# Rearranging the last passes of a two-layer graph network: part of a normalisation moved ahead, two PSUM banks kept across stages, one product moved, one product undivided

## The chip, the cores and the metric

The kernel runs on one core of a Trainium2 chip. The metric is the device time of one execution in microseconds (us), lower is better; the time shown is the median of three runs. A profile is one execution recorded instruction by instruction. In it PE is TensorE's matmul, PEld its weight load, DVE VectorE, ACT ScalarE, POOL GpSimd and SP SyncE, which here only issues transfers.

## The reference

All data is fp32. The batch has 16 samples of 1024 nodes with 256 features.

```
# layer 0
h = maximum(layernorm(x), 0)
A = |  |sigmoid(mean_j - mean_i) - 0.5| - 0.5 | * 2        # mean over features of h
g = relu(h^T @ (adj * A) * para)                           # per sample, 1024 x 1024
k, v = split(h @ kv_w)
x = x + softmax(g^T k * scale) @ v                         # 4 heads of 64
# layer 1
h = maximum(layernorm(x), 0)
A_hat = (adj + I) * dinv[:, None] * dinv[None, :]
z1 = (A_hat @ h) @ W1.T + b1                               # 512 features
h2 = relu(batchnorm(z1))                                   # over all 16 x 1024 rows
z2 = h2 @ W2.T + b2                                        # 256 features
x = x + batchnorm(z2)                                      # over all rows again
```

The two batch normalisations are what stages the end of the kernel. Each needs sums over all 16 samples before its first value can be used.

## The kernel before, in words

The work is in two stages, each inside a block in which the program's own order is the order of every engine's queue (`tc.manual_schedule`). So each of TensorE, VectorE, ScalarE, GpSimd and SP does its instructions in the order in which the code names them, and an instruction that waits holds up everything behind it on its engine.

**Stage 1** (lines 171 to 1222) goes through the 16 samples. For each sample b it computes the graph product, attention (`attention`, L495), and then layer 1's first linear map for the sample before (`linear1_all`, L907: first `linear1`, L693, which multiplies with A_hat, then `linear1_seven`, L794, or for the very last sample `linear1_out`, L883). Both linear maps use a scheme of seven products of blocks for eight, so VectorE forms sums of blocks and ScalarE and VectorE combine the results. The products z1 go to memory in tiles of 512 nodes, `z1_d[t]` with t from 0 to 31, and their statistics for the batch normalisation to `st1`.

`linear1_all` takes hooks, functions that it calls between its products: `first` before the third, `second` after the fourth (`between[1]`, L753), `third` inside `linear1_seven` (`middle`, L861). In the last round (b = 15) these are the functions at L1180 to L1204. They put the layer normalisation of the last sample's x between the products of sample 14: statistics of row blocks 0 to 3 in `first`, of 4 to 7 in `third`, then `norm.invert` (a power on GpSimd for 1/sqrt, L257), a shift on VectorE (L263) and eight relus on ScalarE (L278). `left[3]` to `left[5]` are the last steps of attention. Behind them the products of sample 15 itself run.

[...]In stage 1 three pools hold them: `ps_s` (three buffers of two banks), `ps_o` and `ps_t` (one bank each), all opened at L172 to L174 and closed with the stage.

**Stage 2** (L1225 to L1579) makes z2 and the output. Its pools are opened over the banks that stage 1 left: `ps_x` with four banks and `ps_z` with four (L1246 to L1251). A tile in a bank of a closed pool waits for the last instruction that used the old pool there.

- Tiles t = 0 and 1 go through plain products (`begun`, `plain`, L1393 to L1408). The first half of their relus (`relu_on`, L149: the batch normalisation and the relu in one instruction) stands already in stage 1, between the evictions L900 of the last z1 tiles.
- Then 14 pairs of tiles (`SEVEN`, 1 to 14) go through class `Pair` (L1283), again seven products for eight. `m1`, `m6`, `m5` and `m3` add into one bank x in this order; after each, `keep` copies the sum to SBUF on ScalarE, and the next one waits for that copy. `m2`, `m7` and `m4` go to banks of `ps_z`; `add` and `out` add them on VectorE. While a pair is computed, ScalarE does the relus of the next one. In the last pair there is no next one, and ScalarE does the relus of the last two tiles, 30 and 31, instead (`relu_all`, L1429 and L1437).
- Tiles 30 and 31 then go through four plain products into banks of `ps_x` (L1476 to L1505), output half c = 0 first. Statistics come straight from PSUM. The very last product (tile 31, c = 1) is done in two halves of 256 columns, each with its own statistics; `triples` gathers them with the statistics of all other tiles.
- Meanwhile SP loads the samples' x1 again (`load_x1`, L1232), ten samples ahead in all, into tiles that the pairs have given back. When the second batch normalisation is known, ScalarE and VectorE scale z2, TensorE turns it (L1534), VectorE adds x1 (L1573), and ScalarE's queue stores the sample (L1574). Loads of samples 10 to 15 wait until stores give their tiles back.

Of the kernel before, what the change touches and what calls it, by code (L numbers as in the profile page):

```python
# [10 lines left out]
F32 = mybir.dt.float32  # L11
# [18 lines left out]
def fast_path(  # L30
# [135 lines left out]
    def relu(t, f2):  # L166
        zs[t, f2] = fetch(t, f2)
        relu_on(zs[t, f2], f2)


    with ExitStack() as stage:
        ps_s = stage.enter_context(tc.tile_pool(name="fps_s", bufs=3, space=PSUM))  # L172
        ps_o = stage.enter_context(tc.tile_pool(name="fps_o", bufs=1, space=PSUM))
        ps_t = stage.enter_context(tc.tile_pool(name="fps_t", bufs=1, space=PSUM))  # L174
        big = stage.enter_context(tc.tile_pool(name="fbig", bufs=1))
        two = stage.enter_context(tc.tile_pool(name="ftwo", bufs=2))
        w4 = stage.enter_context(tc.tile_pool(name="fw4", bufs=5))
# [868 lines left out]
        with tc.manual_schedule(engines={ENG.PE, ENG.Activation, ENG.DVE, ENG.Pool, ENG.SP}):  # L1046
# [73 lines left out]
            for b in range(B):  # L1120

                hooks = {}
                if b + 1 < B:
                    for c in range(2):
                        hooks.setdefault(c, []).append(lambda c=c: weights(b + 1, c))
                    if b == 0:
                        for m in range(NC):
                            hooks.setdefault(m // 2, []).append(lambda m=m: column_sums(m))
                        hooks[3].append(roots)
                else:  # L1130
                    w2n = lasting.tile([P, CC, F1], F32, tag="w2n", name="f_w2n")
                    nc.sync.dma_start(w2n, W2.rearrange("(c p) f -> p c f", p=P))
                left = attention(b, *qkv, hooks)

                def more(c):
                    return lambda: weights(b + 1, c)

                norm = Norm(xr[b], f"b{b}")
                between = {
                    0: [  # L1140
                        lambda: turn_h(b + 1), more(2), left[0], left[1], left[2], more(3),
                        left[3], left[4], more(4),
                    ],
                    1: [more(5)],
                    2: [more(6), lambda: norm.stats(0, 4)],
                    3: [more(7)],
                    4: [left[5], lambda: norm.stats(4, NC), norm.invert],
                    6: [lambda: norm.relu(0, 4)],
                    "late": [lambda: norm.relu(4, 6), lambda: norm.relu(6, NC)],
                    8: [lambda: leave(b), lambda: arrive(b + 2)],  # L1150
                }
                if b == 0:
                    scale = [lambda m=m: scale_adj(m) for m in range(NC)]
                    between[3].insert(0, roots_row)
                    between[4] = scale[:3] + between[4] + [scale[3]]
                if b + 1 < B:
                    if 0 < b < B - 2:
                        thirds = load_thirds(b)
                    qkv = graph(b + 1, between)
                    if b == 0:  # L1160
                        for step in scale[4:]:
                            step()
                        thirds = make_thirds(b)
                if b + 2 < B:
                    linear1_all(
                        b,
                        norm.h,
                        thirds,
                        lambda: prepare_start(b + 2),
                        lambda: prepare_end(b + 2),  # L1170
                        lambda: (prepare_row(b + 2), again(b + 1)),
                    )
                elif b + 1 < B:
                    kept_h = norm.h
                    again(b + 1)
                else:

                    w2T = lasting.tile([P, FC, C], F32, tag="w2T", name="f_w2T")

                    def first():  # L1180
                        norm.stats(0, 4)
                        left[3]()
                        left[4]()

                    def second():
                        pass

                    def third():
                        left[5]()
                        norm.stats(4, NC)  # L1190
                        norm.invert()
                        for n, (pool, tag) in enumerate(((ps_o, "o"), (ps_t, "t"))):
                            ps = pool.tile([P, 2, CC, P], F32, tag=tag, name=f"f_w2ps_{n}")
                            for d in range(2):
                                for f in range(CC):
                                    nc.tensor.transpose(
                                        ps[:, d, f, :], w2n[:, f, ts(2 * n + d, P)], ident
                                    )
                            nc.scalar.copy(
                                w2T[:, 2 * n : 2 * n + 2, :].rearrange("p d c -> p (d c)"),  # L1200
                                ps.rearrange("p d f q -> p (d f q)"),
                            )
                        norm.relu(0, NC)
                        leave(b)  # L1204

                    for step in left[:3]:
                        step()
                    thirds = load_thirds(b)
                    def nothing():
                        pass  # L1210

                    made = []
                    linear1_all(
                        b - 1,
                        kept_h,
                        thirds,
                        first,
                        second,
                        third,
                        lambda: made.extend(sums_of_h(b, norm.h)),  # L1220
                    )
                    linear1_all(b, norm.h, thirds, nothing, nothing, nothing, made=made)


    with ExitStack() as stage:  # L1225
# [16 lines left out]
        with tc.manual_schedule(engines={ENG.PE, ENG.Activation, ENG.DVE, ENG.Pool, ENG.SP}):  # L1242
            bn1.affine(FC - 2, FC)

            z2 = big.tile([P, CC, B - 1, N], F32, tag="z2", name="f_z2")
            ps_x = stage.enter_context(tc.tile_pool(name="fps_x", bufs=4, space=PSUM))  # L1246
            zps = ExitStack()
            ps_z = zps.enter_context(tc.tile_pool(name="fps_z", bufs=4, space=PSUM))

            def bank(name, pool=None):  # L1250
                return (pool or ps_z).tile([P, 512], F32, tag="z", name=name)  # L1251
# [138 lines left out]
                    relu_on(zs[t, f2], f2)  # L1390

            pairs = {p: Pair(p) for p in SEVEN}
            begun = {t: [bank(f"f_z2ps_{t}_{c}") for c in range(CC)] for t in (1, 0)}  # L1393
            first = pairs[SEVEN[0]]
            first.load()
            for t in range(2):
# [11 lines left out]
                plain_out(t, begun[t])  # L1408
            first.m1()
            first.keep(0, 0)  # L1410
            for p in SEVEN:
                now, soon = pairs[p], pairs.get(p + 1)
                if p + 2 in pairs:
# [19 lines left out]
                if soon:  # L1433
                    soon.relu(1, 1)
                    soon.relu(1, 0)
                else:
                    relu_all(TT - 1)  # L1437
                now.m5()
                now.keep(1, 1)
                if soon:  # L1440
                    soon.sums13()
                    soon.m1()
                    soon.keep(0, 0)
                now.out(1)
                now.m3()
                now.keep(1, 0)
# [10 lines left out]
            load_x1(AHEAD - 1, [(lasting, "w2n", 1), (io, "x1", None)])  # L1457
            zps.close()
            ps_out = stage.enter_context(tc.tile_pool(name="fps_out", bufs=2, space=PSUM))
            last = {}  # L1460

            triples = big.tile([P, 6, 3], F32, tag="triples", name="f_triples")
            SPLIT = TT // 2
            for k, n in enumerate((SPLIT, TT - 1 - SPLIT)):
                nc.vector.memset(triples[:, k, 0:1], float(n * 512))
# [9 lines left out]
            gather(0, 0, SPLIT)  # L1475
            for c in range(CC):  # L1476
                for t in range(TT - 2, TT):
                    ps = bank(f"f_z2ps_{t}_{c}", ps_x)
                    last[t % 2, c] = ps
                    if c + 1 < CC or t + 1 < TT:  # L1480
                        product(ps, t, c, 0)
                        product(ps, t, c, 2)
                        nc.vector.bn_stats(st2[:, c, t, :], ps)
                        continue
                    gather(1, SPLIT, TT - 1)
                    for k in range(2):
                        at = slice(256 * k, 256 * (k + 1))
                        for f in range(FC):
                            nc.tensor.matmul(
                                ps[:, at],  # L1490
                                w2T[:, f, ts(c, P)],
                                zs[t, f - f % 2][:, f % 2, at],
                                start=(f == 0),
                                stop=(f == FC - 1),
                            )
                        nc.vector.bn_stats(
                            triples[:, 2 + 2 * k : 4 + 2 * k, :].rearrange("p k s -> p (k s)"),
                            ps[:, at],
                        )
                bn2.invert(  # L1500
                    c,
                    c + 1,
# [591 lines left out]
```

## Time and profile before

| | |
|---|---|
| median of 3 runs | 2431.84 us (2431.0 to 2432.97) |
| the profiled execution | 2431.68 us, of which the span is 2429.8 us |
| PE busy | 2387.0 us, 98% of the span |
| DVE, ACT, POOL busy | 1781.9, 1325.6, 308.2 us |
| granted TensorE clock, mean | 0.995 |
| moved by DMA | 275.77 MB, 113 GB/s over the span |
| last products of stage 1 begin | 2124.49 us |
| first product of stage 2 begins | 2163.90 us |
| last product ends; first store is issued | about 2363; 2367.66 us |

Times of instructions are counted from the start of the span. One matmul of the code is two rows in the trace, so a product of 128 x 512 with four matmuls is eight rows. In a row of the timeline, the number in brackets is how long the engine was idle before it, and behind the arrow stands what released it. An "xN" merges N instructions that follow each other.

### The profile page before, as it was taken

The numbers are of one execution on the slowest core, as the hardware profiler recorded it, in microseconds if no ns is written. First come the engines' busy times: TensorE is split into PE (matmuls) and PEld (weight loads), VectorE is DVE, ScalarE is ACT, GpSimd is POOL, SyncE is SP. The second block draws the span as 40 slices with busy tenths as digits, with TensorE's granted clock in tenths as the row PEclk, the third lists the DMA queues.
The fourth block names the chain that finished last, engine by engine and source line by source line (L and its number), as shares of the span: only waits on it lengthen the run. The fifth ranks groups of instructions, "written<-read, shape, count | busy, mean of one in ns | idle before, by whom it ended". The sixth has DMA issues, their size and how long they took to land.

```text
span 2429.8 us, 24669 instructions
## 1 busy us (share of the span) xinstructions
PE 2387.0 (98%) x8042; PEld 1053.3 (43%) x8042; DVE 1781.9 (73%) x2441; ACT 1325.6 (55%) x1932; POOL 308.2 (13%) x546
## 2 busy tenths in 40 slices
PE   8999999999999999999999999999999999999995
PEld 4453444434343434444343434344443434444444
DVE  6878677685949586776859595867768596757766
ACT  6845555464636455554546364545545465346653
POOL 2030202020020302020201103020202010000000
PEclk9999999999999999999999999999999999999997
DMA  5041414232331415142323224141423212355569
GB/s 186 9 140 61 152 61 126 87 91 73 116 94 60 144 61 152 61 126 87 102 67 114 91 63 142 61 151 61 126 87 110 67 61 76 110 209 178 174 225 379
DMA packets 176634, 275.77 MB, mean 113 GB/s; under 512 B 37872, under 2 KB 121328, under 8 KB 176496
## 3 DMA queue, kind: packets, MB, share of 16 engines
q1 hardware_dynamic: 156336, 241.55, 30.6%
q0 software_dynamic: 15552, 15.77, 2.5%
q10 hardware_dynamic: 4608, 16.78, 1.7%
q8 instruction: 66, 1.08, 0.2%
q14 instruction: 72, 0.59, 0.1%
HBM read 169.35 MB, written 71.10 MB: 99 GB/s over the span
## 4 chain that ended last, share of the span: by engine, by line
PE 96%; DMA 2%; DVE 1%; ACT 0%; issue 0%; SPq 0%; POOL 0%; DVEq 0%; ACTq 0%; POOLq 0%
PE f_s L506 19%; PE f_o L547 18%; PE f_gps L398 18%; PE f_aps L703 16%; PE f_zps L809 6%; PE f_vps L423 5%; PE f_zx L1317 4%; PE f_zm L1317 3%; PE f_kpsx L467 2%; PE f_kps L467 1%; DMA out_dram<-f_x1t 1%; PE f_z2ps L1255 1%; PE f_zps L891 1%; PE f_kps L440 1%; PE f_zps3a L809 0%; PE f_zps3b L809 0%
## 5 line engine op out<-in xcount | busy, mean ns | idle before, releaser
L514 ACT ACTIVATE f_p<-f_s 128x1024 f32<-128x1024 f32 x512 | 477.3, 1048 | 150.2 <-PE f_s L506 150.1
L523 DVE TENSOR_TENSOR f_acc<-f_acc,f_p 128x1024 f32<-128x1024 f32 x384 | 470.5, 1225 | 41.1 <-ACT f_w L345 0.5
L506 PE MATMUL f_s<-f_qT,f_kT 64*128 64x512 f32 x2048 | 456.8, 596 | 0.0
L547 PE MATMUL f_o<-f_p,f_v 128*64 128x512 f32 x2048 | 453.6, 595 | 0.0
L398 PE MATMUL f_gps<-f_w,f_h_a 128*128 128x512 f32 x1024 | 444.7, 594 | 0.3 <-DVE f_w L336 0.3
L368 POOL DMA_DIRECT2D f_hT<-f_hQ x480 | 235.8, 499 | 1220.0 <-PE f_gps L398 1170.8
L506 PEld LDWEIGHTS f_s<-f_qT,f_kT 64*128 64x128 f32 x2048 | 190.8, 186 | 263.5 <-ACT f_p L514 117.0
L398 PEld LDWEIGHTS f_gps<-f_w,f_h_a 128*128 128x128 f32 x1024 | 192.8, 190 | 247.0 <-issue 230.7
L547 PEld LDWEIGHTS f_o<-f_p,f_v 128*64 128x64 f32 x2048 | 141.4, 137 | 304.3 <-issue 254.4
L349 DVE SCALAR_TENSOR_TENSOR f_w<-f_w,f_adj 128x1024 f32<-128x1024 f32 x127 | 153.9, 1212 | 38.8 <-ACT f_w L348 38.8
L345 ACT ACTIVATE f_w<-f_row,f_col 128x1024 f32<-128x1024 f32 x127 | 147.0, 1158 | 31.2 <-DMA f_row<-frow 30.2
L278 ACT ACTIVATE f_h_b<-f_x,f_shift_b,f_rstd_b 128x256 f32<-128x256 f32 x128 | 67.8, 594 | 160.9 <-DVE f_shift_b L263 160.9
L348 ACT ACTIVATE f_w<-f_w 128x1024 f32<-128x1024 f32 x127 | 134.3, 1058 | 4.0
L703 PE MATMUL f_aps<-f_ahatT,f_hs 128*128 128x512 f32 x256 | 115.1, 592 | 0.0
L703 PE MATMUL f_aps<-f_ahatT,f_h_b 128*128 128x512 f32 x256 | 112.7, 593 | 0.8 <-DVE f_z L865 0.8
L423 PE MATMUL f_vps<-f_kvw,f_hT 128*128 128x256 f32 x512 | 113.4, 379 | 0.0
L703 PE MATMUL f_aps<-f_t,f_hs 128*128 128x512 f32 x256 | 112.5, 592 | 0.0
L278 ACT ACTIVATE f_h_a<-f_x,f_shift_a,f_rstd_a 128x256 f32<-128x256 f32 x126 | 73.8, 587 | 63.5 <-DVE f_shift_a L263 63.4
L423 PEld LDWEIGHTS f_vps<-f_kvw,f_hT 128*128 128x128 f32 x512 | 97.2, 190 | 20.3 <-issue 7.4
L520 DVE TENSOR_TENSOR f_acc<-f_p,f_p 128x1024 f32<-128x1024 f32 x64 | 76.3, 1192 | 15.3 <-ACT f_p L514 15.3
L589 ACT COPY f_recs<-f_rec 32x32 f32<-32x32 f32 x128 | 31.5, 246 | 98.7 <-DVE f_rec L581 97.5
L574 ACT COPY f_parts<-f_red 32x64 f32<-32x64 f32 x128 | 39.1, 306 | 78.5 <-DVE f_red L539 77.4
(227 smaller groups left out, 2709.7 us busy)
## 6 DMA issues: line engine op xcount, KB each, us to landing
f_t<-ft SPq DMA_DIRECT2D x84, 512.0 KB, 6.9
fz<-f_z SPq DMA_DIRECT2D x64, 512.0 KB, 9.6
f_x<-in_x_dram SPq DMA_DIRECT2D x31, 1024.0 KB, 8.1
f_zb<-fz SPq DMA_DIRECT2D x42, 512.0 KB, 4.3
f_para<-in_L_gnn_para_dram SPq DMA_DIRECT2D x32, 512.0 KB, 4.5
f_att<-f_oT SPq DMA_DIRECT2D x512, 32.0 KB, 1.9
fx<-f_x SPq DMA_DIRECT2D x16, 1024.0 KB, 6.3
f_x1t<-fx SPq DMA_DIRECT2D x32, 512.0 KB, 7.3
```

What stands on the lines that cost most here:

```text
L345: nc.scalar.activation(w, rows[b], AF.Abs, bias=cols[b][:, c : c + 1], scale=0.5 / C)
L349: nc.vector.scalar_tensor_tensor(w, w, 1.0, adj_t[c], ALU.subtract, ALU.mult)
L368: queue.dma_start(to[ts(k, 32), ts(a, 32 * NC)], t[ts(a, 32), k].rearrange("i c r -> i (c r)"),)
L398: nc.tensor.matmul(gps[d][:, ts(g, 512)], hs[b][:, c, ts(d, P)], w[:, ts(g, 512)], start=(c == 0), stop=(c == NC - 1),)
L423: nc.tensor.matmul(ps[:, i, :], hT[e][:, ts(c4 + i, P)], kvw_t[:, e, C : 2 * C], start=(e == 0), stop=(e == CC - 1),)
L506: nc.tensor.matmul(ps[:, e, :], kT[rows_e, pair, ts(m, P)], qT[rows_e, pair, ts(g, 512)], start=True, stop=True,)
L514: nc.scalar.activation(p, ps, AF.Exp)
L523: nc.vector.tensor_add(acc_of[s], acc_of[s], p)
L547: nc.tensor.matmul(o_of[s][e * HD : (e + 1) * HD, :], v[:, m, ts(2 * pair + e, HD)], p[:, e, :], start=(m == 0), stop=(m == NC - 1),)
L703: nc.tensor.matmul(ps, left[:, m, :], right(m), start=not more and m == 0, stop=(m == KH - 1), skip_group_check=more,)
L809: nc.tensor.matmul(ps[i], left[:, ts(i, P)], right, start=not more, stop=True, skip_group_check=more,)
L1317: nc.tensor.matmul(ps, left[:, m, :], right[:, m, :], start=start and m == 0, stop=(m == 1), skip_group_check=not start,)
```

## The change

Four edits, all between the last sample's layer normalisation and the last batch normalisation.

1. The inversion of row blocks 0 to 3 moves from `third` to `first`, and their shift and their four relus to `second`. `third` keeps the other four row blocks.
2. `ps_o` and `ps_t` are opened outside stage 1 and stay open in stage 2; `ps_x` has two banks in place of four. Tile 0's two plain products go to `ps_o` and `ps_t` (`aside`), tile 1's to `ps_z`.
3. In the last pair, tile 31's relus move from ahead of `m5` to behind `keep(1, 1)`, and the first of the four last products (tile 30, c = 0) moves from behind the pair to between `m5` and `m3`. It goes to `ps_o`, the one of tile 31, c = 0 to `ps_t`, the other two to `ps_x`.
4. The last product is done in one piece, with one instruction for its statistics, and `triples` has four entries in place of six.

On SP the order of the instructions is the same as before. TensorE has two product instructions and VectorE one statistics instruction less for edit 4; VectorE and GpSimd have an addition, a shift and a power more for edit 1.

```diff
+    ps_o = ctx.enter_context(tc.tile_pool(name="fps_o", bufs=1, space=PSUM))
+    ps_t = ctx.enter_context(tc.tile_pool(name="fps_t", bufs=1, space=PSUM))
     with ExitStack() as stage:
         ps_s = stage.enter_context(tc.tile_pool(name="fps_s", bufs=3, space=PSUM))
-        ps_o = stage.enter_context(tc.tile_pool(name="fps_o", bufs=1, space=PSUM))
-        ps_t = stage.enter_context(tc.tile_pool(name="fps_t", bufs=1, space=PSUM))
...
                     def first():
                         norm.stats(0, 4)
+                        norm.invert(0, 4)
                         left[3]()
                         left[4]()
                     def second():
-                        pass
+                        norm.shifts(0, 4)
+                        norm.relu(0, 4, False)
                     def third():
                         left[5]()
                         norm.stats(4, NC)
-                        norm.invert()
+                        norm.invert(4, NC)
...
-                        norm.relu(0, NC)
+                        norm.shifts(4, NC)
+                        norm.relu(4, NC, False)
                         leave(b)
...
-            ps_x = stage.enter_context(tc.tile_pool(name="fps_x", bufs=4, space=PSUM))
+            ps_x = stage.enter_context(tc.tile_pool(name="fps_x", bufs=2, space=PSUM))
...
-            begun = {t: [bank(f"f_z2ps_{t}_{c}") for c in range(CC)] for t in (1, 0)}
+            def aside(name):
+                return [
+                    ps_o.tile([P, 512], F32, tag="o", name=f"{name}_0"),
+                    ps_t.tile([P, 512], F32, tag="t", name=f"{name}_1"),
+                ]
+            begun = {0: aside("f_z2ps_0"), 1: [bank(f"f_z2ps_1_{c}") for c in range(CC)]}
...
+            last = {}
+            def last_product(t, c, ps):
+                last[t % 2, c] = ps
+                for f2 in range(0, FC, 2):
+                    product(ps, t, c, f2)
...
                     soon.relu(1, 0)
-                else:
-                    relu_all(TT - 1)
                 now.m5()
                 now.keep(1, 1)
                 if soon:
                     soon.sums13()
                     soon.m1()
                     soon.keep(0, 0)
+                else:
+                    relu_all(TT - 1)
+                    ends = aside("f_z2ps_end")
+                    last_product(TT - 2, 0, ends[0])
                 now.out(1)
                 now.m3()
                 now.keep(1, 0)
...
-            triples = big.tile([P, 6, 3], F32, tag="triples", name="f_triples")
+            triples = big.tile([P, 4, 3], F32, tag="triples", name="f_triples")
...
                 for t in range(TT - 2, TT):
-                    ps = bank(f"f_z2ps_{t}_{c}", ps_x)
-                    last[t % 2, c] = ps
+                    if (t % 2, c) not in last:
+                        last_product(t, c, ends[1] if c == 0 else bank(f"f_z2ps_{t}_1", ps_x))
                     if c + 1 < CC or t + 1 < TT:
-                        product(ps, t, c, 0)
-                        product(ps, t, c, 2)
-                        nc.vector.bn_stats(st2[:, c, t, :], ps)
+                        nc.vector.bn_stats(st2[:, c, t, :], last[t % 2, c])
                         continue
                     gather(1, SPLIT, TT - 1)
-                    for k in range(2):
-                        at = slice(256 * k, 256 * (k + 1))
-                        for f in range(FC):
-                            nc.tensor.matmul(
-                                ps[:, at],
-                                w2T[:, f, ts(c, P)],
-                                zs[t, f - f % 2][:, f % 2, at],
-                                start=(f == 0),
-                                stop=(f == FC - 1),
-                            )
-                        nc.vector.bn_stats(
-                            triples[:, 2 + 2 * k : 4 + 2 * k, :].rearrange("p k s -> p (k s)"),
-                            ps[:, at],
-                        )
+                    nc.vector.bn_stats(
+                        triples[:, 2:4, :].rearrange("p k s -> p (k s)"), last[t % 2, c]
+                    )
```

More of the change, by code (lines that the diff above doesn't have):

```diff
@@ L1459, in fast_path @@
             ps_out = stage.enter_context(tc.tile_pool(name="fps_out", bufs=2, space=PSUM))
-            last = {}
-            triples = big.tile([P, 6, 3], F32, tag="triples", name="f_triples")
+            triples = big.tile([P, 4, 3], F32, tag="triples", name="f_triples")
             SPLIT = TT // 2
```

## The prediction, made before the changed kernel was run

> **What bounds the kernel now.** I read the chain of waits first, because it says which engine carries the end.
>
> ```profile
> PE 96%; DMA 2%; DVE 1%; ACT 0%; issue 0%; SPq 0%; POOL 0%; DVEq 0%; ACTq 0%; POOLq 0%
> ```
>
> 96% of the span is TensorE working or being waited for by itself, so only two things can move the time here: a hole in TensorE's row, or the transfers after it. I then read TensorE alone in order of time from 2080 us on, where the edits lie, and looked for holes.
>
> ```profile
> 2124.49 7.11 PE L703 MATMUL f_aps<-f_ahatT,f_h_b 128*128 128x512 f32 x16 [0.83 <-DVE f_z L865]
> ...
> 2148.60 13.90 PE L891 MATMUL f_zps<-f_aggT,f_w1T 128*128 128x512 f32 x32
> 2163.90 14.00 PE L1255 MATMUL f_z2ps<-f_z,f_w2T 128*128 128x512 f32 x32 [1.40 <-ACT f_z L900]
> ...
> 2341.17 1.88 PE L1317 MATMUL f_zx<-f_zb,f_w2s 128*128 128x512 f32 x4
> 2344.82 1.99 PE L1317 MATMUL f_zx<-f_zb,f_w2s 128*128 128x512 f32 x4 [1.77 <-ACT f_z L1328]
> 2346.64 1.88 PE L1317 MATMUL f_zm<-f_zt,f_w2T 128*128 128x512 f32 x4
> 2348.35 10.46 PE L1255 MATMUL f_z2ps<-f_z,f_w2T 128*128 128x512 f32 x24
> 2358.65 1.89 PE L1489 MATMUL f_z2ps<-f_z,f_w2T 128*128 128x256 f32 x8
> 2361.07 1.99 PE L1489 MATMUL f_z2ps<-f_z,f_w2T 128*128 128x256 f32 x8 [0.52 <-DVE f_triples L1496]
> ```
>
> Columns: start, busy us, engine, line, operation, then in brackets the idle time and its releaser. There are exactly four holes before the output stage: 0.83, 1.40, 1.77 and 0.52 us. One matmul of the code is two rows here; 24 rows take 2358.65 - 2348.35 = 10.30 us, so a row is 0.429 us and one 128x512 product (four matmuls) 3.43 us. A modelled end runs on past the next start, so I count holes by rows: 2148.60 + 32 x 0.429 = 2162.33, and the second hole is really 1.57 us; in the same way the third is 2344.82 - (2341.17 + 1.72) = 1.93 us.
>
> The first hole hangs on VectorE, which sits behind GpSimd's power:
>
> ```profile
> 2119.73 0.17 DVE L256 TENSOR_SCALAR f_var_b<-f_mv_b 128x8 f32<-128x8 f32 x1
> 2121.72 0.17 DVE L263 SCALAR_TENSOR_TENSOR f_shift_b<-f_mv_b,f_rstd_b 128x8 f32<-128x8 f32 x1 [1.81 <-POOL f_rstd_b L257]
> 2121.80 1.22 DVE L864 TENSOR_TENSOR f_z<-f_z,f_zps 128x1024 f32<-128x1024 f32 x1
> 2123.13 1.22 DVE L865 TENSOR_TENSOR f_z<-f_z,f_zps 128x1024 f32<-128x1024 f32 x1
> ```
>
> L864 and L865 need nothing from the shift; they only stand behind it. The third hole is on ScalarE:
>
> ```profile
> 2339.65 0.58 ACT L1328 COPY f_z<-f_zx 128x512 f32<-128x512 f32 x1 [1.74 <-PE f_zx L1317]
> 2340.13 1.52 ACT L152 ACTIVATE f_z<-f_z,f_bn_t,f_bn_s 128x512 f32<-128x512 f32 x2
> 2342.78 1.52 ACT L152 ACTIVATE f_z<-f_z,f_bn_t,f_bn_s 128x512 f32<-128x512 f32 x2 [1.13 <-DMA f_z<-fz]
> 2344.20 0.56 ACT L1328 COPY f_z<-f_zx 128x512 f32<-128x512 f32 x1
> ```
>
> The copy at 2344.20 is keep(1, 1), which TensorE's m3 waits for; it stands behind the relus of the last tile, whose data landed at 2342.78. After the products, transfers decide, as windows of 5 us show (last two columns: busy share of the DMA engines, GB/s):
>
> ```profile
> 2355.00:2360.00 5.00, 5.00 (x16) 2.71 (x15) 3.61 (x9) 1.52 (x2) 0.55 (x1) 1.00 1.04 413
> 2360.00:2365.00 5.00, 3.41 (x19) 2.52 (x17) 2.11 (x10) 3.11 (x3) 0.55 (x1) 1.00 0.85 315
> 2365.00:2370.00 5.00, 3.28 (x24) 2.57 (x24) 4.16 (x6) 2.77 (x3) 0.00 (x0) 1.00 0.63 235
> ...
> 2375.00:2380.00 5.00, 4.09 (x32) 3.42 (x32) 4.88 (x6) 3.01 (x3) 0.00 (x0) 1.00 1.02 397
> ```
>
> Loads of x1 fill the engines until about 2361; a dip follows until the first stores (2367.66); from 2375 to 2425 every window is at 397 to 420 GB/s. So the end is the start of the stores plus a fixed amount of traffic.
>
> [...]both halves of the last product are in one bank, and the trace shows the second half waiting 0.52 us for the first half's statistics. [...]0.52 granted from 2390 to 2405 among holes of 1.8 to 3.3 us, while the holes above left it at 1.00.
>
> **The change, part by part.**
>
> *A. Half of the relus ahead.* Statistics of the first four row blocks exist at 2096. The change inverts them there and runs four relus (8 took 4.04, so 2.0 us) on ScalarE after the shift. The shift stands on VectorE behind L752 (2100.51 + 0.69); its power was done near 2097, so VectorE doesn't stall on it; the relus run from about 2101.4 to 2103.5, in ScalarE's idle 5.25 us before L755 at 2103.94. Cover gone, L755 would be late, but its reader on TensorE comes 3.43 us later: nothing. In the late part GpSimd's power is 4 wide instead of 8: the two 4-wide ones at the start of this trace took 1.05 us, the 8-wide here 1.64. Shift, L864 and L865 move up by 0.58, L865 ends at 2123.77, TensorE starts at 2123.91. The last old row ends at 2122.64 + 2 x 0.429 = 2123.50, so 0.4 of the hole stays. The copy L868 behind the relus comes 2.5 us earlier, so it isn't late. Gain 0.58; bounds 0.3 and 0.99.
>
> *B. Two banks kept.* Before, the first z2 matmul takes over banks of pools that have just closed, and waits for the last eviction L900 (2162.59 + 1.26). With ps_o and ps_t alive its tile waits for its own relu alone: ScalarE's two relus from 2161.08 end by 2162.60, the first half near 2161.85, before TensorE is free at 2162.33; the second half is needed 0.86 later. Hole gone: 1.57. What is late next, in the times of before with the hole closed (A moves all of it alike): tile 1's matmuls begin two products' halves later, at 2165.76, and its relus and its banks, which still wait for L900, are ready at 2165.25; tile 0's second half is wanted at 2169.19 and 2170.05, its relus end near 2168.7 and at 2169.45; m1 begins at 2176.06 and m2 at 2177.78, and pair 1's relus end at 2176.55. ScalarE's four copies then end at 2178.52 and keep(0, 0) at 2179.1, where m6 wants it at 2179.5. All fit, the narrowest by 0.4 us. Pair 1's loads wait on VectorE's aggregate (SP issues them at 2166.54), not on TensorE, and land just ahead of ScalarE, as before. ps_x with two buffers for four costs nothing: a pair's bank is free one whole pair (12 us) before it is taken again. Gain 1.57; bounds 0.6 (the first pair gives a microsecond back) and 1.57.
>
> *C. Product between copy and relus.* keep(1, 1) now follows m5 directly, and TensorE has 3.43 us of product (tile 30's relus ended at 2337.9) while ScalarE copies (0.58) and does tile 31's relus (3.0). Both are over before m3 and the second product need them; tile 31's data has landed by then. The product is only moved, so its time is saved nowhere else. The hole of 1.93 goes, and 0.10 of restart (m3's four rows took 1.82 for 1.72). Gain 2.03; bounds 1.5 and 2.03. Its bank in ps_o was last read by tile 0's copies, 160 us before.
>
> *D. Last product in one piece.* Before: from the end of the third product, 2358.65, to the final aggregate at 2363.57 is 4.92 us (two halves, 0.52 of hole, two restarts, statistics 0.43). After: 3.43 + 0.21 until VectorE starts (as at 2351.99) + 0.74 until the next (as 2355.42 to 2356.16) = 4.38. Gain 0.54; bounds 0.3 and 0.7. The wider statistics instruction costs 0.27 and is in this sum. VectorE is free: tile 30's second statistics and gather end 1.6 us before.
>
> Sum of the stores' start: 0.58 + 1.57 + 2.03 + 0.54 = 4.72 us. SP's queue keeps its order. Its loads of x1 follow the last z load, which waits for m2 of the last pair (2337.97), so they start only A + B = 2.15 earlier; the four that reuse the last z tiles come 3 to 5 earlier, as their products do. The 2.57 between loads and stores is taken from the dip: missing rate in 2360 to 2370 is (100 + 180) x 5 / 415 = 3.4 us. It holds. Some 0.5 us of loads may still run when stores begin, and can cost up to that.
>
> Profiled execution: 2431.68 (span 2429.8), less 4.72, is 2426.96; the median of the runs is 0.16 higher, so 2427.1.
>
> **The rivals.**
> 1. *First pair gives B back.* ScalarE's row is solid from 2167.99 to 2178.52 and its loads land just ahead; then TensorE stalls at m2 or m6 for what B saved. For it: margins of 0.4. Against: ScalarE idled 1.13 us before keep(0, 0). 2427.1 + 1.57 = 2428.7.
> 2. *Transfers decide.* If stores gain nothing on the loads, the end moves by 2.15: 2429.7. For it: DMA at 1.03 in the tail. Against: the dip of 3.4 us.
> 3. *More than the sum*: A's hole closes wholly (0.4 more) and C and D save more of the restarts (0.3): 2426.4. Against it: L865's end at 2123.77, by rows that the trace shows.
> 4. *Slower.* [...]the trace holds 17 us at half clock in the tail. If such a stretch fell into the products instead, it would cost 8.5 us: 2427.1 + 8.5 = 2435.6. [...]the change only removes holes there, and holes up to 1.93 left the clock at 1.00. Unlikely.
> That an edit does nothing is open only for B; in the built program its wait is on the relu and no longer on L900.
>
> **How the numbers follow.** Forecast 0.66, rivals in order 0.12, 0.08, 0.09, 0.05. Time 2427.1. The range 2426.0 to 2429.8 holds all but rival 4 and tails. 0.2%, about what a measurement of this kernel can tell, is 4.86 us, a line at 2426.98: the forecast straddles it, so I give it 0.32 faster and 0.34 same. Faster: 0.32 + 0.09 = 0.41. Same: 0.34 + 0.12 + 0.08 + 0.01 = 0.55. Slower: 0.04, most of rival 4.
>
> **What would show it.** A: power 1.05 us, next hole about 0.4. B: first f_z2ps row with no idle time before it. C: m3 directly after a product. D: one row group of 512 columns. Then first stores near 2363, and the dip about 1 us. It is wrong if f_zm or f_zx rows of the first pairs show idle time over 0.5 us, or the stores start earlier and the end doesn't.

## The result, and the profile after

| | before | after |
|---|---|---|
| median of 22 runs each | 2432.19 us (2430.5 to 2434.8) | 2427.43 us (2425.95 to 2429.78) |
| profiled execution (span) | 2431.68 (2429.8) us | 2427.43 (2425.5) us |
| first products of the last linear map begin | 2124.49 us | 2122.78 us |
| stage 2's first product begins | 2163.90 us | 2160.65 us |
| loads of x1, from sample 1 on, begin | 2338.33 us | 2334.98 us |
| TensorE's row that starts with the first store | 2367.68 us | 2361.72 us |

The ratio is 0.998, 95% interval 0.9974 to 0.9986: 4.76 us less, with 3.4 to 6.3 in the interval. In the profile of after, the chain of waits still ends in TensorE:

```profile
PE 96%; DMA 2%; DVE 0%; issue 0%; SPq 0%; ACT 0%; ACTq 0%; DVEq 0%; POOLq 0%; POOL 0%
```

TensorE in order of time, with the places of the four old holes:

```profile
2122.78 7.13 PE L704 MATMUL f_aps<-f_ahatT,f_h_b 128*128 128x512 f32 x16
...
2146.92 13.90 PE L892 MATMUL f_zps<-f_aggT,f_w1T 128*128 128x512 f32 x32
2160.65 13.90 PE L1259 MATMUL f_z2ps<-f_z,f_w2T 128*128 128x512 f32 x32
...
2339.53 3.60 PE L1259 MATMUL f_z2ps_end<-f_z,f_w2T 128*128 128x512 f32 x8
2342.97 1.88 PE L1321 MATMUL f_zx<-f_zb,f_w2s 128*128 128x512 f32 x4
2344.68 1.88 PE L1321 MATMUL f_zm<-f_zt,f_w2T 128*128 128x512 f32 x4
2346.40 3.60 PE L1259 MATMUL f_z2ps_end<-f_z,f_w2T 128*128 128x512 f32 x8
2349.83 7.03 PE L1259 MATMUL f_z2ps<-f_z,f_w2T 128*128 128x512 f32 x16
2356.70 1.04 PE L1541 MATMUL f_outps<-f_ident,f_z 128*128 128x128 f32 x8
2359.75 1.09 PE L1541 MATMUL f_outps<-f_ident,f_z 128*128 128x128 f32 x8 [2.02 <-DVE f_z L1523]
2361.72 4.38 PE L1541 MATMUL f_outps<-f_ident,f_z 128*128 128x128 f32 x24 [0.88 <-DVE f_x1t L1580]
```

None of the rows from 2122.78 to 2349.83 has a bracket: the holes of 0.83, 1.40, 1.77 and 0.52 us are gone. 2160.65 - 2146.92 = 13.73 us is exactly 32 rows of 0.429, so even the half hidden part of the second hole went. What stands out is the last row: 24 transposes take 4.38 us there, where a row of 16 took 2.22 in before:

```profile
2367.68 2.22 PE L1534 MATMUL f_outps<-f_ident,f_z 128*128 128x128 f32 x16 [0.88 <-DVE f_x1t L1573]
```

This row starts with the first store: both wait for VectorE's first addition of x1 (the store is issued at 2367.66 before and 2361.70 after).

Not all of the 5.96 us between these two rows is the change's. A row of 16 matmuls in `linear1` for sample 14 (f_t, f_hs, at 2093.44 before and 2092.52 after) stands ahead of every edited instruction and is already 0.92 us earlier; over the profiles of this study it lies between 2092.30 and 2093.66. So below I count from that row, the *mark*. From the mark, the first store's row came 5.04 us earlier (269.20 for 274.24), and the start of the loads 2.43.

The transfers, in the windows of before (the last three columns: granted clock, busy share of the DMA engines, GB/s):

```profile
2355.00:2360.00 5.00, 2.98 (x15) 1.74 (x14) 2.23 (x8) 3.82 (x5) 0.55 (x1) 1.00 1.02 408
2360.00:2365.00 5.00, 4.12 (x24) 3.79 (x22) 3.58 (x3) 2.88 (x3) 0.00 (x0) 0.66 0.90 358
2365.00:2370.00 5.00, 4.38 (x34) 3.43 (x32) 4.77 (x5) 2.61 (x3) 0.00 (x0) 1.00 0.83 247
2370.00:2375.00 5.00, 3.87 (x30) 3.27 (x31) 4.88 (x6) 1.87 (x3) 0.00 (x0) 1.00 1.03 349
2375.00:2380.00 5.00, 2.63 (x21) 1.97 (x20) 4.88 (x5) 2.36 (x3) 0.00 (x0) 1.00 1.02 412
```

The dip is still there. Counted from 2360 to 2380 as rate missing to 415 GB/s (both profiles hold 410 to 420 in every window from 2380 to 2415) it is (57 + 168 + 66 + 3) x 5 / 415 = 3.5 us, against (100 + 180 + 77 + 18) x 5 / 415 = 4.5 in the same windows of before. And the clock is at 0.66 in the window in which the stores begin, where before had 1.00.

### The profile page after: what moved, and what is told of

It reads as the page before. It is cut to its first block, busy times and chain, and to the rows that moved or that the text cites. A ratio compares the mean times of both kernels' runs of the same rounds, so it can differ in the third digit from the quotient of the medians.

```text
span 2425.5 us, 24656 instructions
## 1 busy us (share of the span) xinstructions
PE 2385.3 (98%) x8034; PEld 1052.4 (43%) x8034; DVE 1781.4 (73%) x2442; ACT 1325.2 (55%) x1932; POOL 308.5 (13%) x547
## 4 chain that ended last, share of the span: by engine, by line
PE 96%; DMA 2%; DVE 0%; issue 0%; SPq 0%; ACT 0%; ACTq 0%; DVEq 0%; POOLq 0%; POOL 0%
PE f_s L507 19%; PE f_o L548 19%; PE f_gps L399 18%; PE f_aps L704 16%; PE f_zps L810 6%; PE f_vps L424 5%; PE f_zx L1321 4%; PE f_zm L1321 3%; PE f_kpsx L468 2%; PE f_kps L468 1%; DMA out_dram<-f_x1t 1%; PE f_z2ps L1259 1%; PE f_zps L892 1%; PE f_kps L441 1%; PE f_zps3b L810 1%; PE f_zps3a L810 1%
```

## The experiments

My theory was that of the prediction: the end follows the stores' start one for one, and the four gains add up. The rival: transfers decide, so only what starts the loads of x1 earlier (A and B) counts. Each kernel but the last (e12) is the changed one with one edit; e8 has none and e10 two. Medians scatter by about 1.5 us in an interval, as much as an edit is worth, so I read single edits from TensorE's rows as well. "Second transposes" is the row of 8 that VectorE's last scaling releases, at 272.27 us from the mark before and 267.23 after.

### Undoing one part

**e1, without A.**
```diff
-                        norm.invert(0, 4)
...
-                        norm.shifts(0, 4)
-                        norm.relu(0, 4, False)
+                        pass
...
-                        norm.invert(4, NC)
+                        norm.invert()
...
-                        norm.shifts(4, NC)
-                        norm.relu(4, NC, False)
+                        norm.relu(0, NC)
```


> The changed kernel with edit 1 undone (all eight relus late). Two theories of the end stand against each other in these four runs. Stores: the end moves one for one with the start of the stores, so each undone edit costs its own hole. Traffic: the end moves with the start of the x1 loads, and the dip between loads and stores takes up whatever comes after that. Here both say: the hole of about 0.8 us behind VectorE's L866 is back before the last products of stage 1 and everything after it is 0.8 later than in the changed kernel; time about 0.8 above it, some 4.0 below the kernel before (ratio 0.9984). The hole before the first f_z2ps row stays away.

Measured 2428.87 us, ratio 0.9986 (0.9979 to 0.9992). The old hole is back, 0.83 us behind VectorE's L866, and the second transposes come 0.75 us later than in after.

**e2, without B.**
```diff
-    ps_o = ctx.enter_context(tc.tile_pool(name="fps_o", bufs=1, space=PSUM))
-    ps_t = ctx.enter_context(tc.tile_pool(name="fps_t", bufs=1, space=PSUM))
...
+        ps_o = stage.enter_context(tc.tile_pool(name="fps_o", bufs=1, space=PSUM))
+        ps_t = stage.enter_context(tc.tile_pool(name="fps_t", bufs=1, space=PSUM))
...
-            ps_x = stage.enter_context(tc.tile_pool(name="fps_x", bufs=2, space=PSUM))
+            ps_x = stage.enter_context(tc.tile_pool(name="fps_x", bufs=4, space=PSUM))
```
`aside` takes two banks of `ps_x`, for the last products alone; tile 0's products go to `ps_z` again, as before.

> The changed kernel with edit 2 undone: ps_o and ps_t close with stage 1, ps_x has four banks, the moved product goes to one of them. Both theories: 1.4 us idle (1.55 by rows) before the first f_z2ps row, released by the eviction L900, and nothing else changed; time about 1.55 above the changed kernel, 3.2 below the kernel before (0.9987). If the first pair had given something back in the changed kernel, the cost would be under 1.2.

Measured 2429.92 us, ratio 0.999 (0.9983 to 0.9996). The hole of 1.41 us is back behind ScalarE's eviction; second transposes 1.67 us later.

**e3, without C.**
```diff
+                else:
+                    relu_all(TT - 1)
                 now.m5()
                 now.keep(1, 1)
...
-                else:
-                    relu_all(TT - 1)
-                    ends = aside("f_z2ps_end")
-                    last_product(TT - 2, 0, ends[0])
...
+            ends = aside("f_z2ps_end")
+            last_product(TT - 2, 0, ends[0])
```


> The changed kernel with edit 3 undone: tile 31's relus ahead of m5 again, the first last product after the pair, still in ps_o. The loads start as in the changed kernel, the stores 2.0 us later, with 1.8 us idle before m3. Stores: time 2.0 above the changed kernel, 2.7 below the kernel before (0.9989). Traffic: no more than 0.5 above the changed kernel (0.9982).

Measured 2430.42 us, ratio 0.9992 (0.9986 to 0.9999); second transposes 1.80 us later. By the traffic theory C is worth nothing; by its interval and its row it is worth most of what was forecast. ScalarE's row shows why it is 1.80 and not 2.03:

```profile
2337.63 1.52 ACT L152 ACTIVATE f_z<-f_z,f_bn_t,f_bn_s 128x512 f32<-128x512 f32 x2
2340.04 1.52 ACT L152 ACTIVATE f_z<-f_z,f_bn_t,f_bn_s 128x512 f32<-128x512 f32 x2 [0.90 <-DMA f_z<-fz]
2341.47 0.56 ACT L1332 COPY f_z<-f_zx 128x512 f32<-128x512 f32 x1
```

The relus ahead of the copy waited 0.90 us for their data; in the profile of before they waited 1.13. The length of this hole is partly the moment at which a load lands.

**e4, without D.**
```diff
-            triples = big.tile([P, 4, 3], F32, tag="triples", name="f_triples")
+            triples = big.tile([P, 6, 3], F32, tag="triples", name="f_triples")
...
+                    for k in range(2):
+                        at = slice(256 * k, 256 * (k + 1))
```
with the two half products and their statistics as before.

> The changed kernel with edit 4 undone: the last product in two halves of 256 columns, six triples. 0.5 us idle between the halves, stores 0.55 later, loads as in the changed kernel. Stores: time 0.55 above the changed kernel, 4.2 below the kernel before (0.9983). Traffic: nothing lost (0.9980).

Measured 2427.94 us, ratio 0.9982 (0.9975 to 0.9989): the median can't tell it from after. By the rows it is worth what was forecast: the wait of 0.52 us between the halves is back, and the second transposes come 0.56 us later.

The four rows together, 0.75 + 1.67 + 1.80 + 0.56 = 4.78 us, make up nearly all of the 5.04.

### Stores or traffic

**e5 and e11, stores late.** The last statistics are computed six times over; the result is the same.
```diff
+LATE = 6
...
-                    nc.vector.bn_stats(
+                    for n in range(LATE):
+                        nc.vector.bn_stats(
...
```


> The changed kernel with the statistics of the last product taken six times instead of once, into the same place (five times 0.62 us more on VectorE before the last aggregate; the result is the same). Loads as in the changed kernel, stores 3.1 us later. Stores: time 3.1 above the changed kernel, 1.6 below the kernel before (0.9993). Traffic: at most 1.5 above the changed kernel, since the dip grows instead (0.9986).

Measured 2432.08 us, ratio 1.0001 (0.9993 to 1.0009). The five further statistics delay the second transposes by 3.67 us (3.1 had been expected); the ratio rose by 0.0021, which is 5.1 us. So the end follows the stores, and by these numbers by more than one for one, though the intervals of this run and of after leave one for one possible. Traffic alone is out.

**e6, loads held.** A small store on SP that reads a later copy of the last pair holds the loads of x1 back (what it writes is not read).
```diff
-                    for n in range(1, AHEAD - 3):
-                        load_x1(n)
...
                 now.keep(0, 1)
+                if not soon:
+                    nc.sync.dma_start(z1_d[0][:, 0, 0:32], place(now.t[0], 1)[:, 0:32])
+                    for n in range(1, AHEAD - 3):
+                        load_x1(n)
```


> The changed kernel with SP's loads of x1 for samples 1 to 6 (and all behind them) held back until keep(0, 1) of the last pair, by a small store of 16 KB that reads what this copy writes. Loads start about 2.2 us later, stores as in the changed kernel. Stores: no change (within 0.5 us of the changed kernel, 0.9980). Traffic: time 2.2 above the changed kernel (0.9989).

Measured 2427.6 us, ratio 0.9983 (0.9976 to 0.999). The loads begin at 2338.24, 2.3 us later by the mark than in after, and the stores as in after. About 0.7 us of it shows in the ratio, but the interval holds what both theories expected, 0.998 and 0.9989, so this run doesn't decide between them. The dip is smaller:

```profile
2360.00:2365.00 5.00, 3.27 (x24) 2.57 (x24) 4.16 (x6) 2.82 (x3) 0.00 (x0) 1.00 1.02 409
2365.00:2370.00 5.00, 4.37 (x32) 3.43 (x32) 4.94 (x5) 3.81 (x4) 0.00 (x0) 1.00 1.07 352
```

The windows that had 358 and 247 GB/s in after hold 409 and 352 here. That need not be the late loads' doing: the clock is at 1.00 here, though TensorE's waits of 2.01 and 0.88 us are those of after. The next experiments show how much of the dip is the clock's.

### The clock at the stores' start

After's profile had one thing that the prediction did not: half clock as the stores began. If that costs time, it would explain both the dip that stayed and e5's surplus.

**e7 and e9, clock kept.** Twelve idle transposes stand in the hole of 2 us, in which TensorE waits for the last scaling; they write columns that later transposes overwrite.
```diff
+WARM = 12
...
                     for h in range(NH):
                         turn_out(0, h, 0, outs[h])
+                    for n in range(WARM):
+                        nc.tensor.transpose(
+                            outs[n % 2][:, n // 2 % 4, ts(1, P)], ident, ident
+                        )
```


> The changed kernel with twelve idle transposes of the identity on TensorE in the hole before the second half of sample 0's output transposes, into columns that the next transposes overwrite. They take about 1.3 us of the 2.0 us hole and delay nothing. If the half clock seen at 2361.7 to 2365.1 in the changed kernel's profile comes from this hole and costs time at the end, the clock stays at 1.00 from 2355 to 2370, sample 0's and 1's adds follow each other without the 0.93 us wait, and the time is up to 1.5 below the changed kernel (0.9974 to 0.9980). If transfers alone set the end once the stores run, there is no change (0.9980).

Measured 2426.68 us, ratio 0.9981 (0.9973 to 0.9988). Its profile ended 1.9 us before that of after, but that execution was the fastest of its 15, and the ratio shows nothing. That was inconclusive, so I ran after itself (e8), the same edit (e9), e5's kernel (e11), and e5's kernel with 48 idle transposes in its longer hole (e10) on one chip:

> The changed kernel once more, as the mark for the three runs beside it. Both theories: ratio to the kernel before 0.998 as measured, some 4.7 us under it; the first stores 60 to 64 us ahead of the end of the span, at half clock for one stretch of 3.4 us when they begin.

> 12 idle transposes in TensorE's hole ahead of the last two row blocks of column 1, as in e7. Clock theory (the half clock when the stores begin costs time): in the profiles the tail from the first store's transposes to the end was 63.8 us in the changed kernel and 62.1 us in e7, so this run should end 1.7 us before e8, ratio 0.9973. Rival (transfers decide the tail, whatever TensorE's clock): within 0.3 us of e8, ratio 0.998.

> The last statistics 6 times, as in e5, which puts the stores off by 3.7 us in its profile, and 48 idle transposes (about 0.11 us each, 5.3 us) in the hole that this leaves, so that the clock stays at 1.00. Clock theory: e5 lost more than 3.7 us to the changed kernel because its hole of 5.7 us halved the clock; here the loss is 3.7 us less what the clock gives, so 1.7 us or more under e11, ratio 0.9988 or less. Rival: the same as e11 within 0.5 us.

> e5 once more on the same chip as e8. Stores theory: one for one with its stores' start, 3.7 us above e8, ratio 0.9995. If e5's median stands (5 us lost), ratio 1.0001, and the surplus of 1.3 us is the clock's by the clock theory, noise between chips by the rival.

| kernel | median | ratio, interval |
|---|---|---|
| e8, after | 2427.76 us (2426.55 to 2429.78) | 0.9979, 0.9971 to 0.9987 |
| e9, after, clock kept | 2426.41 us (2425.93 to 2427.27) | 0.9974, 0.9965 to 0.9984 |
| e11, late | 2432.53 us (2431.01 to 2434.45) | 1.0, 0.9992 to 1.0009 |
| e10, late, clock kept | 2430.39 us (2429.93 to 2433.75) | 0.9991, 0.9983 to 1.0 |

The profiles of e9 and e10 have the clock at 1.00 in every window from 2355 to 2380; e11's has 0.73 and 0.58 in the two from 2360. With the clock kept, after is 1.35 us faster and the late kernel 2.14 us. With the clock kept in both, putting the stores off by 3.7 us costs 2430.39 - 2426.41 = 3.98 us, about one for one; without, 4.77. The ratios' intervals overlap within each pair, but all 10 runs of e9 lie below the median of e8, 12 of e10's 13 lie below every run of e11, and both pairs' profiles point the same way. The executions without a profile have a mean granted clock each: in e8 the 5 runs at 0.994 or 0.995 took 2428.9 us on average, the 8 at 0.996 or 0.997 2427.0; in e9 these groups are alike, 2426.5 and 2426.6. That fits a clock that is halved for longer in some executions, but it is a mean over the whole span and doesn't say where.

In e8's profile the clock was halved longer than in after's:

```profile
2361.45 1.10 PE L1541 MATMUL f_outps<-f_ident,f_z 128*128 128x128 f32 x8 [2.01 <-DVE f_z L1523]
2363.42 6.53 PE L1541 MATMUL f_outps<-f_ident,f_z 128*128 128x128 f32 x32 [0.87 <-DVE f_x1t L1580]
```

32 transposes took 6.53 us here. In e9 the same place looks like this, first TensorE, then the windows:

```profile
2357.96 1.47 PE L1560 MATMUL f_outps<-f_ident 128*128 128x128 f32 x12
2360.13 1.09 PE L1542 MATMUL f_outps<-f_ident,f_z 128*128 128x128 f32 x8 [0.70 <-DVE f_z L1524]
2362.10 2.22 PE L1542 MATMUL f_outps<-f_ident,f_z 128*128 128x128 f32 x16 [0.88 <-DVE f_x1t L1585]
```

```profile
2360.00:2365.00 5.00, 3.77 (x28) 3.06 (x29) 4.20 (x5) 2.88 (x4) 0.00 (x0) 1.00 0.84 334
2365.00:2370.00 5.00, 3.89 (x31) 2.97 (x29) 4.95 (x6) 3.41 (x4) 0.00 (x0) 1.00 1.01 325
2370.00:2375.00 5.00, 4.26 (x32) 3.38 (x32) 4.88 (x5) 2.43 (x3) 0.00 (x0) 1.00 1.02 410
```

The transposes are back at 2.22 us for 16, and 2370 to 2375 is full (410 for 349 GB/s). Between the two stands VectorE, whose additions of x1 release the stores. In after an addition waited 0.93 us for transposes at half clock; in e9 the first six follow each other without a wait in between:

```profile
2363.73 1.22 DVE L1580 TENSOR_TENSOR f_x1t<-f_x1t,f_outps 128x1024 f32<-128x1024 f32 x1 [0.93 <-PE f_outps L1541]
```

```profile
2360.83 7.17 DVE L1585 TENSOR_TENSOR f_x1t<-f_x1t,f_outps 128x1024 f32<-128x1024 f32 x6 [0.75 <-PE f_outps L1542]
```

e9 has the lowest ratio of the study; it is one edit beyond the change.

**e12, the kernel before with the same 12 transposes.**

> The kernel before with the same 12 idle transposes in the same hole (1.77 us there). The profile of the kernel before shows the clock at 1.00 from 2360 to 2375 us. Theory one, the kernel before loses nothing at this place: ratio 1.000, within 0.4 us. Theory two, in other executions its clock is halved there too, and it loses what the changed kernel loses (1.35 us in the pair e8 and e9) or a good part of it: 0.7 to 1.4 us faster, ratio 0.9994 to 0.9997. Theory two would be needed to make the sums meet: 5.04 us earlier stores less 1.35 us of half clock is 3.7 us, and 4.76 us were measured.

Measured 2431.64 us, ratio 0.9998 (0.999 to 1.0006), 0.26 us under before. That is nearer theory one, but the interval holds both theories, so it is not decided whether before loses clock here. Its runs hint that it does in some executions: of the 17 runs of before measured beside it, the 2 at a mean clock of 0.994 took 2433.9 us on average, the 10 at 0.995 2432.6 and the 5 at 0.996 2431.4; of the 13 with transposes none is at 0.994, and those at 0.995 and 0.996 took 2431.8 and 2432.0.

Its profile has the kernel before's products a second time, and there the third hole was 1.21 us in place of 1.77, because tile 31's data came sooner (ScalarE waited 0.57 us for it, not 1.13). So the start of the stores in before moves by half a microsecond from run to run.

### One sum for all

One sum fits all the profiles. Missing is the rate missing to 415 GB/s in 2360 to 2380, as worked out above:

| kernel | loads begin | missing | end of span | end - loads - missing |
|---|---|---|---|---|
| before | 2338.33 | 4.5 | 2429.8 | 87.0 |
| after | 2334.98 | 3.5 | 2425.5 | 87.0 |
| e8 | 2336.68 | 4.0 | 2427.5 | 86.8 |
| e6, loads held | 2338.24 | 1.8 | 2427.3 | 87.3 |
| e7, clock kept | 2334.75 | 2.0 | 2423.6 | 86.9 |
| e9, clock kept | 2335.36 | 2.1 | 2424.3 | 86.8 |
| e10, late, clock kept | 2335.77 | 6.0 | 2428.9 | 87.1 |
| e11, late | 2335.74 | 7.7 | 2431.2 | 87.8 |

(e1 to e5 and e12 lie at 86.6 to 87.4.) The end is the start of the loads, about 87 us of transfers, and what is missing around the stores' start. This is bookkeeping, as the traffic is practically the same in all: it says where the time went, not why, and it scatters by 1.2 us. The profiled executions aren't all typical either: e7's was the fastest of its 15, e8's the second slowest of 13, e6's the slowest of 19.

What makes the missing part is shown by the experiments: late stores (e5 with 7.3 and e11 with 7.7, after with 3.5) and slow transposes (7.7 in e11 against 6.0 in e10, 4.0 in e8 against 2.1 in e9). Later loads give little of it back. e6, e7 and e9 all have the clock at 1.00 from 2355 to 2375 and the stores alike from the mark; e6's loads start 2.3 us later, yet only 0.2 to 0.3 us less is missing, and its profile ends 2.5 us later (333.9 us from the mark for 331.3 and 331.4). By the medians, e6 is 0.92 us above e7, which was measured beside it; a part of that can be the clock in e6's other executions. So the stores' start is not all that counts: 1.8 to 2.1 us stay missing in these three. That they would stay missing with still earlier stores, and that then only an earlier start of the loads would help, is my estimate from these three profiles; no run shows it.

## Why the prediction was right, and where not

The time forecast was 2427.1 us and 2427.43 was measured, and the four edits did what was said of them. Point by point:

- **A**, forecast 0.58, was 0.79 at its own hole. The power took 1.01 us where 1.05 had been taken for it, and VectorE's wait for it fell from 1.81 to 1.12 us; TensorE then began 0.05 us after L866's end, where I had carried over 0.14. VectorE's rows:

```profile
2120.10 0.17 DVE L264 SCALAR_TENSOR_TENSOR f_shift_b<-f_mv_b,f_rstd_b 128x4 f32<-128x4 f32 x1 [1.12 <-POOL f_rstd_b L258]
2120.18 1.22 DVE L865 TENSOR_TENSOR f_z<-f_z,f_zps 128x1024 f32<-128x1024 f32 x1
2121.51 1.22 DVE L866 TENSOR_TENSOR f_z<-f_z,f_zps 128x1024 f32<-128x1024 f32 x1
```

  L866 ends at 2122.73. The last old row ends at 2121.78 + 0.86 = 2122.64, so 0.14 of hole stays where 0.4 was forecast. A small term, mis-sized.
- **B**, forecast 1.57: the first product follows without a hole, and undoing it costs 1.67. The narrow margin that was named, `keep(0, 0)` before m6, is real: in e8's profile a load landed late (ScalarE waited 0.81 us for f_zb), and m6 waited for that copy.

```profile
2173.93 1.52 ACT L152 ACTIVATE f_zb<-f_zb,f_bn_t,f_bn_s 128x512 f32<-128x512 f32 x2 [0.81 <-DMA f_zb<-fz]
...
2178.76 0.61 ACT L1332 COPY f_z<-f_zx 128x512 f32<-128x512 f32 x1
```

```profile
2179.42 1.98 PE L1321 MATMUL f_zx<-f_zt,f_w2s 128*128 128x512 f32 x4 [0.38 <-ACT f_z L1332]
```

  This row of TensorE is m6; it began at 2179.42 where 2178.88 was due, and with the restart (the four rows of m6 took 1.82 us, the next four 1.72) that execution gave back 0.63 us. So rival 1 is not false: it happened in one of the profiled executions, and for a part of B.
- **C**, forecast 2.03: 1.80 in e3. The forecast took the hole of one execution for its size; 1.21 to 1.77 us of idle time were seen in before's two profiles.
- **D**, forecast 0.54: 0.56.
- **The sum**, 4.72 forecast for the stores' start, was 5.04 from the mark. The loads, forecast 2.15 earlier, were 2.43, most of the difference being A's (0.21).
- **"The 2.57 between loads and stores is taken from the dip ... It holds."** This is the step that failed in size. In e7 and e9 it does hold: missing falls from 4.5 to 2.0 and 2.1, as 4.5 - 2.57 says. (The dip of "about 1 us" was counted from 2360 to 2370 alone, 3.4 us, and left out the 1.1 us that are missing from 2370 to 2380.) In after as it is, half clock puts 1.4 to 1.9 us back (3.5 in its profile, 4.0 in e8). Rival 4 looked for half clock in the wrong place, in the products, took "holes up to 1.93 left the clock at 1.00" for safety, and didn't ask about the output stage, where the only matmuls between holes are short transposes (8 in 1.09 us between waits of 2.02 and 0.88 in after). There keeping the clock was worth 1.35 us (e8 and e9) and 2.14 us (e11 and e10), not 8.5. What makes the clock fall had not been shown then, and these runs don't show it either. "The end is the start of the stores plus a fixed amount" takes the tail's rate as given: 410 to 420 GB/s in every window from 2380 to 2415, before and after, was measured; that it could not be higher was not shown. It also leaves the loads out: held back in e6, with the stores in their place, they seem to have cost something, 0.7 us by the ratio, though within the intervals.

With this step off, the median should have come out above the forecast, and did by only 0.3 us. By its profile the change brought 2.43 of earlier loads and 0.98 of smaller dip, 3.4 us, which is the lower end of the measured interval of 3.4 to 6.3; the other 0.9 us of that profile stood ahead of every edited instruction. e8's profile, counted from the mark, ends only 2.45 us before that of before. The medians say more: 4.76 us, and 4.81 again in e8 (3.2 to 7.1). Why they say more is open. It could be that before loses clock as well in executions that were not profiled, as e12's runs hint. So that the forecast was met to 0.3 us, with a loss of one or two that it didn't have, is in part luck. It also stays open why e7's ratio showed nothing where e9's pair showed 1.35 us: e7's median was 0.75 us below after's, but the kernel before, measured beside it, was 0.77 us faster too.

## What to carry to other kernels

Before a saved wait is booked, write down what the end is made of: here the start of the loads, fixed traffic, and what is missing around the stores' start, so each edit is worth what it takes from the first or the last. When holes are closed, look also at the short matmuls that come after them: here 8 transposes between waits of 2.0 and 0.9 us went with half clock for 3.4 us in after and 6.8 us in e8, and with none in e6. With 12 idle transposes in the first wait the clock stayed at 1.00 from 2355 to 2380 in e7 and e9, and e9's median is 1.35 us below e8's. Take a hole's size from several executions if a load ends it, since one profile shows one landing time: tile 31's data was waited for 1.13 us in before and 0.57 us in e12.

## What the runs showed of the hardware

- The clock at the stores' start differs from execution to execution, and half clock came in portions of 3.4 us. In after the granted clock was 0.50 in every window of 0.25 us from 2361.50 to 2364.50; a clock of 0.66 in one window of 5 us is 0.34 x 5 / 0.5 = 3.4 us at half clock. With the same waits of 2.0 and 0.9 us around 8 transposes, it was halved for 3.4 us in after, e1 and e2, for 6.8 us in e8 (0.74 and 0.58 in two windows), and not at all in e6. Further on, before's four windows from 2390 to 2410 (0.56, 0.50, 0.50, 0.74) make 17.0 us, five such portions. What starts one is not shown: after's clock fell at about 2361.3 us, behind the 8 transposes from 2359.75 to 2360.84, and TensorE's longest hole from 2122.78 us up to there was 2.02 us.
- Half clock went with lost transfers, not only with slow matmuls: e8 with 32 transposes at 6.53 us misses 4.0 us of transfers, e9 with 16 at 2.22 us misses 2.1. In e1, with 3.4 us at half clock, only 2.6 were missing, so the size of the loss is not fixed.
